# Other edge prices and durations in a kernel's own planner: scores behind scores, and the begins of GpSimd and VectorE pieces

## The chip, the cores and the metric

The kernel runs on one core of a Trainium2 chip. The metric is device time in microseconds (us) of one execution; lower is better. Times are medians of several executions.

## The reference, cut to what matters

32 sequences of 256 tokens with 128 channels pass through a feed-forward network (`ffn`), an attention over channels, and the same feed-forward network again, all in float32:

```python
x = x + 0.5 * ffn(layernorm(x))
x = x + channel_attention(layernorm(x))   # softmax(q^T k / sqrt(8)) over channels, 16 heads
x = x + 0.5 * ffn(layernorm(x))
# ffn: two layers of
h = shift_token(x)                        # second half of the channels from the token before
q, k, v = split(h @ wqkv)                 # 8 heads of 64
q, k = rotary_xpos(l2norm(q) * qs, l2norm(k) * ks)
x = x + local_attention(q, k, v) @ wo     # each block of 64 sees itself and the block before
h = layernorm(shift_token(x)) * lg + lb
a, g = split(h @ w1 + b1)
x = x + (a * gelu(g)) @ w2 + b2
```

## The kernel before

One sequence is two tiles of 128 tokens (t = 0 and 1). Each layer of each sequence is cut into pieces, each of which runs on one engine:

- `shifted_T` (L173): TensorE transposes the normalised x (L179), two copies put it into hT, one token late for half of the channels.
- `project` (L186): TensorE makes q and k (L198, 1024 columns, into a two-bank PSUM place called "wide") and v (L232, into a one-bank place called "bank"). ScalarE squares (L204), VectorE multiplies by the cosine and sine tables (L206, L209) and sums the squares (L215), GpSimd makes the norms (L219, L125), adds (L223) and scales (L226).
- TensorE transposes q and k (`transposed`, L141); ScalarE or VectorE copies them out (L131).
- `scores` (L240): TensorE writes the scores of one t into a "wide" place. They are 64 small matmuls on parts of the array (L264, 64 x 32) and a mask on the whole array (L252). For t = 0 the mask comes first, for t = 1 last. VectorE takes the maximum and subtracts it (L275, L278), ScalarE takes the exponential (L281).
- `attended` (L284): the probabilities are transposed (L141), 32 small products with the values go into a "wide" place (L303, parts of the array of 96 x 32), VectorE divides (L310, L311).
- `attention_out` (L318): a transpose (L141) and a product (L326), VectorE adds (L331).
- `gated_mlp` (L377): SP moves half of the channels by one token in three copies on chip (L381, L382); `layernorm` (L147) takes statistics on VectorE (L153, L154), their scale on GpSimd (L157 to L160) and the normalisation on ScalarE (L164); then z is transposed, TensorE makes three hidden pieces (L395), ScalarE the gelu (L403), VectorE the gate (L410), TensorE the output (L421).
- `channel_attention` (L451) is a chain of small products (L465, L477, L503) and a softmax.

There are two "wide" and four "bank" places in PSUM. Up to eight sequences are under way at once (`CHAINS`, L33).

No loop sets the order of the pieces. Class `Plan` (L656) does, when the kernel is built. Every `plan.op` names the engine, a duration in us, what it follows, and the places that it uses. `Plan.order` (L718) plays the pieces against clocks of its own for the five engines, looks 30 TensorE pieces ahead, tries 16 orders with small random delays, and keeps five pieces of the one with the least idle time of TensorE. Then each engine's instructions are issued in the order found, and semaphores do the waiting on the chip.

Three tables enter that play. `SYNC` (L663) is what an engine needs to begin after another engine's piece. `TAIL` (L664) is how long after a piece its result is there. `CHANGE` (L666) is added to TensorE's begin by the form that the array was left in and the form that the next piece begins with: "all", "parts" (scores) or "values". Scores of t = 0 have the form ("all", "parts"), scores of t = 1 ("parts", "all") (L273), attended values ("values", "values") (L307). `begin` (L776) adds it:

```python
t = max(o.given[engine], self.clock[engine] + self.CHANGE.get((self.array, o.form[0]), 0.0))
```

and `go` (L805) sums `t - self.clock["PE"]` up as TensorE's idle time, so that a negative entry counts as time won. The duration of t = 0 scores is given as 1.35 us and that of t = 1 scores as 1.16 (L272).

Of the kernel before, what the change touches and what calls it, by code (L numbers as in the profile page):

```python
# [40 lines left out]
def kernel(ctx: ExitStack, tc: tile.TileContext, ins: dict, out: bass.AP):  # L41
    nc = tc.nc
    x = ins["x"]
# [34 lines left out]
    plan = Plan()  # L78
# [45 lines left out]
    def rsqrt(dst, src, n):  # L124
        nc.gpsimd.tensor_tensor(dst, src, mhalf[:, :n], ALU.pow)  # L125
# [21 lines left out]
    def layernorm(src, x, kind, after):  # L147

        st, mv, var, rstd, shift, y = (plan.take(k) for k in ("st", "mv", "v1", "v1", "v1", kind))

        def stats(e):
            for t in range(NT):
                nc.vector.bn_stats(st.t[:, t, :], src(t))  # L153
                nc.vector.bn_aggr(mv.t[:, t, :], st.t[:, t, :])  # L154

        def scale(e):
            nc.gpsimd.tensor_scalar_add(var.t, mv.t[:, :, 1], EPS)  # L157
            rsqrt(rstd.t, var.t, NT)
            nc.gpsimd.tensor_mul(shift.t, mv.t[:, :, 0], rstd.t)
            nc.gpsimd.tensor_scalar_mul(shift.t, shift.t, -1.0)  # L160

        def norm(e):
            for t in range(NT):
                nc.scalar.activation(  # L164
                    y.t[:, t, :], src(t), AF.Identity, bias=shift.t[:, t : t + 1], scale=rstd.t[:, t : t + 1]
                )

        a = plan.op("DVE", 0.84, stats, after, [x, st, mv, var, rstd, shift, y])
        b = plan.op("POOL", 1.6, scale, [a], [mv, var, rstd, shift])
        c = plan.op("ACT", 0.79, norm, [b], [x, rstd, shift, y])  # L170
        return y, c
# [205 lines left out]
    def gated_mlp(l, y1, after):  # L377
# [5 lines left out]

        moved = plan.op("SP", 2.15, shift, after, [y1], late=2.0)
        z, n = layernorm(lambda t: y1.t[:, t, 0:2, :].rearrange("p a d -> p (a d)"), y1, "z", [moved])
        zT, uT, y2 = (plan.take(k) for k in ("zT", "uT", "y"))
        _, q = transposed(lambda: [z.t[:, t, :] for t in range(NT)], NT, lambda: zT.t, zT, [n], [z])
# [49 lines left out]
    def ffn(x, after):  # L437

        y, d = layernorm(lambda t: x.t[:, t, :], x, "y", after)
        for l in range(DEPTH):  # L440
            y1, done = local_attention(l, y, [d])
            y, d = gated_mlp(l, y1, done)
        xn = plan.take("x")
        e = plan.op(
            "DVE", 0.35,
            lambda e: nc.vector.scalar_tensor_tensor(xn.t, y.t, 0.5, x.t, ALU.mult, ALU.add), [d], [x, y, xn],
            apart=True,
        )
        return xn, [e]

    def channel_attention(x, after):  # L451


        xn, d = layernorm(lambda t: x.t[:, t, :], x, "y", after)
        xT = plan.take("xT")
        _, tr = transposed(lambda: [xn.t[:, t, :] for t in range(NT)], NT, lambda: xT.t, xT, [d], [xn])
# [142 lines left out]
    def make_hidden(l, after):  # L599

        pb = plan.take("bank")

        def mm(e):
            for a in range(2):
                for j, (c0, n) in enumerate(HCH):
                    i = a * len(HCH) + j
                    nc.tensor.matmul(
                        pb.t[:n, i : i + 1], w1[:, l, a * HID + c0 : a * HID + c0 + n],
                        lnb[:, l : l + 1], start=True, stop=True,
                    )  # L610

        def add(e):
            sums = pb.t[:, : 2 * len(HCH)].rearrange("p (a j) -> p a j", a=2)
            for n, js in ((P, slice(0, 2)), (HCH[2][1], slice(2, 3))):
                nc.vector.tensor_add(b1[:n, l, :, js], b1[:n, l, :, js], sums[:n, :, js])

        m = plan.op("PE", 2.0, mm, after, [pb])
        return [
            plan.op("DVE", 0.2, add, [m], [pb]),
            plan.op("DVE", 0.6, lambda e: nc.vector.tensor_scalar_mul(w1[:, l, :], w1[:, l, :], lng[:, l : l + 1]), [m], []),  # L620
        ]
# [3 lines left out]
    def prepare():  # L625

        raw = plan.take("qk")
        t = plan.op("ACT", 1.5, lambda e: load_tables(*tables(raw)), [], [raw], late=4.5)
        first = plan.op("SP", 0.5, lambda e: load_wqkv(0), [], [], late=6.0)
        cast = plan.op("DVE", 0.2, lambda e: nc.vector.tensor_copy(identh, ident), [], [])  # L630
        made["tables"] = [[make_tables(l, raw, [t])] for l in range(DEPTH)]
        made["masks"] = make_masks(made["tables"][0] + made["tables"][1] + [cast])
        plan.rank = 2.3
        hidden = plan.op("SP", 5.5, lambda e: load_hidden(), [], [], late=8.0)
        plan.rank = 3.3
        second = plan.op("SP", 0.5, lambda e: load_wqkv(1), [], [], late=6.0)
        rest = plan.op("SP", 3.0, lambda e: load_rest(), [], [], late=8.0)
        plan.rank = 0
        made["hidden"] = [make_hidden(l, ([hidden], [hidden, rest])[l]) for l in range(DEPTH)]
        made["weights"], made["more"] = [[first], [second]], [[hidden], [rest]]  # L640

    for g in range(x.shape[0]):
        plan.rank, plan.base = g, len(plan.ops)
        xt, seq = plan.take("x"), plan.take("sequence")
        a = plan.op("SP", 0.5, lambda e, xt=xt, g=g: nc.sync.dma_start(xt.t, xg[g]), [], [xt, seq], late=2.5)
        if g == 0:
            prepare()
        xo, a = ffn(xt, [a])
        xo, a = channel_attention(xo, a)
        xo, a = ffn(xo, a)  # L650
# [5 lines left out]
class Plan:  # L656
# [3 lines left out]

    SYNC = {"PE": 0.16, "DVE": 0.08, "ACT": 0.08, "POOL": 0.09, "SP": 0.08}  # L663
    TAIL = {"PE": 0.165, "ACT": 0.105, "DVE": 0.085, "POOL": 0.04, "SP": 0.0}  # L664

    CHANGE = {("all", "parts"): 0.09, ("all", "values"): 0.09, ("values", "values"): -0.11}  # L666
    RATHER = 1.0
    TABLE = 1.3
    TURNS = ("wide", "bank")
# [106 lines left out]
    def begin(self, o, engine):  # L776

        t = max(o.given[engine], self.clock[engine], self.clock["POOL"] if o.apart else 0.0)
        if engine == "PE":
            t = max(o.given[engine], self.clock[engine] + self.CHANGE.get((self.array, o.form[0]), 0.0))  # L780
        sync = self.SYNC[engine]
        for p in o.uses:
# [22 lines left out]
    def go(self, until, later, chance):  # L805
# [16 lines left out]
        while heap and (until is None or self.through < until):  # L822
# [44 lines left out]
            for d in o.then:  # L867
                self.undo.append((d, {"wait": d.wait}))
                d.wait -= 1
                if not d.wait:  # L870
                    d.given = {
                        e: max(x.done[0] + (self.SYNC[e] if x.done[1] != e or x.late else 0.03) for x in d.after)
                        for e in d.engines
# [52 lines left out]
```

## Time and profile before

| what | us |
|---|---|
| median of three timed runs | 2786.19 |
| their lowest and highest | 2784.39, 2789.49 |
| the profiled execution | 2782.01 |
| its span in the profile | 2780.2 |
| TensorE busy with matmuls | 2732.8 |
| GpSimd, VectorE, ScalarE busy | 2215.1, 2125.3, 1977.0 |

The mean granted TensorE clock of the span is 0.998. The profile shows one execution. Busy columns count instructions, not waits. Matmuls are pipelined: one begins before the one ahead of it has ended, so in a timeline the difference of two starts tells how long a piece holds TensorE, and the busy column (second figure) is longer than that. In a row of stretches, the columns after the stretch and its length are the busy time of TensorE's matmuls, its weight loads, VectorE, ScalarE and GpSimd, each with its count of instructions, then the granted clock, the share of the DMA engines and GB/s.

### The profile page before, as it was taken

The page shows a single profiled execution, that of the slowest core. Times are in us where ns is not written, and L with a number is a line of the kernel's source. Part 1 is how long each engine was busy: PE and PEld are TensorE (multiplying, and loading weights), DVE is VectorE, ACT ScalarE, POOL GpSimd, SP SyncE. Part 2 cuts the span into 40 slices and gives each one's busy share as a digit, 9 for nine tenths or more (in the row PEclk, how much of TensorE's full clock was granted, in tenths as well). Part 3 has the DMA queues.
Part 4 walks back from the last instruction along what each step waited for, and adds up shares of the span by engine and source line. Part 5 has one row for each costly group of instructions (what it writes and reads, how often), then busy time and mean ns, then how long its engine had stood idle before and what let it go on. Part 6 is the DMA issues. An engine that isn't in the chain of part 4 may idle for free.

```text
span 2780.2 us, 106518 instructions
## 1 busy us (share of the span) xinstructions
PE 2732.8 (98%) x46200; PEld 2116.9 (76%) x46200; DVE 2125.3 (76%) x3762; ACT 1977.0 (71%) x3595; POOL 2215.1 (80%) x1972
## 2 busy tenths in 40 slices
PE   7999999999999999999999999999999999999999
PEld 4777778778777777777877777777787777778677
DVE  6788777777787777777878778777877788776776
ACT  5777767767677777767677777677766677677666
POOL 8888887888787788787868979788779788684884
PEclk9999999999999999999999999999999999999999
DMA  3112111212112111112111121221111121111111
GB/s 104 40 36 53 41 44 44 54 38 64 42 41 53 34 40 49 48 41 55 44 50 39 38 52 50 52 53 43 38 48 41 47 52 46 43 49 31 41 48 40
DMA packets 125585, 129.68 MB, mean 47 GB/s; under 512 B 56592, under 2 KB 75452, under 8 KB 125116
## 3 DMA queue, kind: packets, MB, share of 16 engines
q1 hardware_dynamic: 124300, 122.47, 16.9%
q8 instruction: 363, 5.95, 0.9%
q14 instruction: 106, 0.87, 0.1%
q10 hardware_dynamic: 816, 0.39, 0.0%
HBM read 8.00 MB, written 4.19 MB: 4 GB/s over the span
## 4 chain that ended last, share of the span: by engine, by line
PE 92%; DVE 3%; POOL 2%; issue 1%; ACT 1%; DMA 1%; SPq 0%; POOLq 0%; DVEq 0%; ACTq 0%
PE ps_bank L141 21%; PE ps_wide L198 15%; PE ps_bank L395 11%; PE ps_wide L303 9%; PE ps_bank L326 8%; PE ps_wide L264 8%; PE ps_bank L232 7%; PE ps_bank L421 6%; PE ps_wide L252 3%; PE ps_bank L465 1%; PE ps_bank L179 1%; POOL rn L125 1%; PE ps_bank L503 1%; DMA y<-y 0%; DVE cp L494 0%
## 5 line engine op out<-in xcount | busy, mean ns | idle before, releaser
L223 POOL TENSOR_TENSOR qk<-qk,sq 128x1024 f32<-128x1024 f32 x256 | 606.8, 2371 | 243.3 <-DVE sq L209 120.6
L125 POOL TENSOR_TENSOR rn<-ssq,mhalf 128x16 f32<-128x16 f32 x256 | 748.4, 2923 | 21.3
L226 POOL TENSOR_TENSOR qk<-qk,rn 128x1024 f32<-128x1024 f32 x256 | 487.5, 1906 | 13.7
L198 PE MATMUL ps_wide<-wqkv,hT 128*128 128x512 f32 x1024 | 487.2, 598 | 2.9 <-DVE pr L278 2.1
L206 DVE TENSOR_TENSOR qk<-ps_wide,tab 128x1024 f32<-128x1024 f32 x256 | 312.3, 1220 | 191.9 <-ACT sq L204 115.4
L395 PE MATMUL ps_bank<-zT,w 128*128 128x256 f32 (+1 forms) x1536 | 372.9, 381 | 1.7 <-ACT zT L131 1.1
L204 ACT ACTIVATE sq<-ps_wide 128x1024 f32<-128x1024 f32 x256 | 262.4, 1025 | 140.0 <-PE ps_wide L198 93.3
L131 ACT COPY pT<-ps_bank 96x512 f32<-96x512 f32 x508 | 283.3, 585 | 93.8 <-PE ps_bank L141 89.1
L209 DVE TENSOR_TENSOR sq<-ps_wide,tab 128x1024 f32<-128x1024 f32 x256 | 311.0, 1215 | 45.2 <-PE ps_wide L198 28.4
L215 DVE TENSOR_REDUCE ssq<-sq 128x16 f32<-128x1024 f32 x256 | 309.7, 1210 | 35.0 <-ACT sq L204 34.6
L395 PEld LDWEIGHTS ps_bank<-zT,w 128*128 128x128 f32 (+1 forms) x1536 | 259.3, 178 | 64.5 <-issue 12.7
L198 PEld LDWEIGHTS ps_wide<-wqkv,hT 128*128 128x128 f32 x1024 | 180.7, 191 | 146.2 <-issue 134.8
L141 PE MATMUL ps_bank<-ident,qk 128*128 128x128 f32 x2048 | 286.0, 275 | 1.4 <-POOL qk L226 1.2
L275 DVE TENSOR_REDUCE mx<-ps_wide 128x8 f32<-128x768 f32 x256 | 242.9, 949 | 57.8 <-PE ps_wide L252 30.8
L141 PE MATMUL ps_bank<-ident,pr 128*96 128x128 f32 x2048 | 286.3, 274 | 0.3
L303 PE MATMUL ps_wide<-vm,pT 96*32 96x65 f32 x8192 | 273.8, 221 | 3.5 <-issue 2.5
L326 PEld LDWEIGHTS ps_bank<-wo,oT 128*128 128x128 f32 x2048 | 252.5, 192 | 29.4 <-issue 19.7
L303 PE MATMUL ps_wide<-vt,pT 96*32 96x65 f32 x8192 | 272.4, 220 | 1.8 <-issue 1.7
L326 PE MATMUL ps_bank<-wo,oT 128*128 128x128 f32 x2048 | 270.6, 276 | 0.8 <-ACT oT L131 0.8
L141 PEld LDWEIGHTS ps_bank<-ident,pr 128*96 128x96 f32 x2048 | 229.5, 126 | 48.7 <-issue 31.8
L232 PE MATMUL ps_bank<-wqkv,hT 128*128 128x512 f32 x512 | 261.3, 603 | 5.2 <-DVE uT L410 2.1
L141 PEld LDWEIGHTS ps_bank<-ident,qk 128*128 128x128 f32 x2048 | 234.8, 141 | 37.8 <-issue 20.9
(102 smaller groups left out, 5266.4 us busy)
## 6 DMA issues: line engine op xcount, KB each, us to landing
vm<-vt SPq DMA_DIRECT2D x256, 195.0 KB
vm<-vt SPq DMA_DIRECT2D x256, 130.0 KB
vm<-vt SPq DMA_DIRECT2D x256, 65.0 KB
y<-y SPq DMA_DIRECT2D x128, 56.0 KB
x<-in_x SPq DMA_DIRECT2D x32, 128.0 KB
out<-x SPq DMA_DIRECT2D x32, 128.0 KB
y<-y SPq DMA_DIRECT2D x128, 7.5 KB
y<-y SPq DMA_DIRECT2D x128, 0.2 KB
```

Of the source, the lines that this page charges most:

```text
L125: nc.gpsimd.tensor_tensor(dst, src, mhalf[:, :n], ALU.pow)
L141: nc.tensor.transpose(pt.t[:rows, j * P : (j + 1) * P], src, ident)
L198: nc.tensor.matmul(wide.t[:, a], lhsT(), wqkv[:, l, a * INNER : (a + 1) * INNER], start=True, stop=True)
L206: c = plan.op("DVE", 1.14, lambda e: nc.vector.tensor_mul(qk.t, pq(), cos), [m] + made["tables"][l], [wide, qk])
L209: lambda e: nc.vector.tensor_mul(sn.t.rearrange(five, x=2), pq().rearrange(five, x=2)[:, :, :, ::-1, :], sin.rearrange(five, x=2)),
L215: "DVE", 1.13, lambda e: nc.vector.tensor_reduce(ssq.t, sq.t, AX.X, ALU.add), [s], [sq, ssq]
L223: f = plan.op("POOL", 2.42, lambda e: nc.gpsimd.tensor_add(qk.t, qk.t, sn.t), [c, i], [qk, sn])
L226: lambda e: nc.gpsimd.tensor_mul(qk.t, qk.t, rn.t.unsqueeze(3).to_broadcast([P, 2, HEADS, DH])),
L232: lambda e: nc.tensor.matmul(mv.t, lhsT(), wqkv[:, l, 2 * INNER :], start=True, stop=True),
L303: nc.tensor.matmul(o()[q, r, j, :], pTs[r].t[:FR, j, q], v[:, 2 * j + r, :], start=True, stop=True)
L326: nc.tensor.matmul(pw.t[:, :P], oT.t[:, j, :], wo[:, l, j, :], start=j == 0, stop=j == PAIRS - 1)
L395: nc.tensor.matmul(pa.t[:w, i * SEQ : (i + 1) * SEQ], w1[:, l, i * HID + c0 : i * HID + c0 + w], zf(), start=True, stop=True,)
```

## The change

Five numbers of the planner are other ones. No piece, engine, tile or place is added or taken away; the planner finds another order with them, on every engine and in SP's queue. The statistics of `layernorm` are counted at 0.95 us instead of 0.84, the TensorE piece of `make_hidden` (twelve one-column products for the bias sums, run twice at the start) at 1.15 instead of 2.0, the begin of a GpSimd piece behind another engine's at 0.15 instead of 0.09, and scores that follow scores in the form "parts" have an entry of their own in `CHANGE`, where there was none (0.0).

```diff
-        a = plan.op("DVE", 0.84, stats, after, [x, st, mv, var, rstd, shift, y])
+        a = plan.op("DVE", 0.95, stats, after, [x, st, mv, var, rstd, shift, y])
...
-        m = plan.op("PE", 2.0, mm, after, [pb])
+        m = plan.op("PE", 1.15, mm, after, [pb])
...
-    SYNC = {"PE": 0.16, "DVE": 0.08, "ACT": 0.08, "POOL": 0.09, "SP": 0.08}
+    SYNC = {"PE": 0.16, "DVE": 0.08, "ACT": 0.08, "POOL": 0.15, "SP": 0.08}
...
-    CHANGE = {("all", "parts"): 0.09, ("all", "values"): 0.09, ("values", "values"): -0.11}
+    CHANGE = {("all", "parts"): 0.09, ("all", "values"): 0.09, ("values", "values"): -0.11, ("parts", "parts"): -0.18}
```

## The prediction

> **What bounds the kernel now.** I read the page first, for the bound; then the chain of waits on it; then the busy time by stretches; last TensorE's timeline, because the change is about single edges between TensorE pieces.
>
> ```profile
> span 2780.2 us, 106518 instructions
> PE 2732.8 (98%) x46200; PEld 2116.9 (76%) x46200; DVE 2125.3 (76%) x3762; ACT 1977.0 (71%) x3595; POOL 2215.1 (80%) x1972
> PE 92%; DVE 3%; POOL 2%; issue 1%; ACT 1%; DMA 1%; SPq 0%; POOLq 0%; DVEq 0%; ACTq 0%
> ```
>
> TensorE is busy 98% of the span and carries 92% of the chain that ended last; no other engine is above 80%. So time goes only if TensorE's own pieces follow each other faster, or if its waits shrink. Next, where TensorE waits (PE busy is the third figure of a row):
>
> ```profile
> 0.00:100.00 100.00, 83.58 (x1107) 55.98 (x1108) 65.53 (x125) 60.46 (x108) 86.77 (x127) 0.97 0.30 85
> 100.00:2500.00 2400.00, 2380.43 (x40685) 1850.68 (x40685) 1865.04 (x3268) 1728.10 (x3138) 1946.04 (x1673) 1.00 0.18 46
> 2580.00:2600.00 20.00, 17.87 (x130) 11.32 (x129) 13.52 (x27) 12.77 (x27) 18.52 (x21) 0.91 0.15 38
> ```
>
> Start: 16.4 us idle in 100. Middle: 19.6 idle in 2400. The last 280 us: 11.2 idle. The middle is nearly full, so waits there can hardly give more than some microseconds. What remains are the edges:
>
> ```profile
> 1002.56 1.00 PE L264 MATMUL ps_wide<-kT,qT 64*32 64x96 f32 x64
> 1003.49 1.08 PE L141 MATMUL ps_bank<-ident,pr 128*96 128x128 f32 x8
> ...
> 1016.27 1.88 PE L198 MATMUL ps_wide<-wqkv,hT 128*128 128x512 f32 x4
> 1017.99 0.60 PE L141 MATMUL ps_bank<-ident,ob 128*128 128x128 f32 x4
> ```
> ```profile
> 1005.27 1.88 PE L198 MATMUL ps_wide<-wqkv,hT 128*128 128x512 f32 x4
> 1007.08 0.75 PE L264 MATMUL ps_wide<-kT,qT 64*32 64x96 f32 x43
> ```
> ```profile
> 1090.07 1.73 PE L264 MATMUL ps_wide<-kT,qT 64*32 64x96 f32 x128
> 1091.73 0.39 PE L252 MATMUL ps_wide<-mask,identh 128*128 128x256 bf16 x2
> ```
>
> Read starts, not busy times. A first-half score block (t=0, it ends in the small array parts) that a transpose follows holds TensorE 0.93 us from its first L264 (1002.56 to 1003.49). A projection before a whole-array piece takes 1.72 (1016.27 to 1017.99); before a second-half score block (t=1, it begins in the parts) it takes 1.81 (1005.27 to 1007.08). At 1090 the two blocks stand together: 128 score matmuls take 1.66, where two apart take 2 x 0.93.
>
> **The edges, over all records.** From start to start, medians where nothing waits: the last matmul of t=0 to the next piece is 172 ns (117 edges), to a t=1 block 2 ns (11 edges). A t=1 block or an attended-values block costs 93 ns more to enter after a whole-array piece (202 against 109 after a transpose, 522 against 429 after a projection), and nothing more after a t=0 or a values block. Values to values is 36 ns, values to anything else 148, and the second of two such blocks is 24 ns shorter inside (876 against 900). So the new price of -0.18 is a real edge: 172 - 2 = 170 ns, and the pair saves the 93 of entry besides.
>
> **What the change does.** It adds and removes no matmul. It gives the planner another price for one edge and four other durations, and the whole order comes out otherwise. I counted the order of instructions of both kernels, which no run is needed for:
> - t=0 directly followed by t=1: 11 before, 58 after (of 128). +47 x 0.170 = **8.0 us** less.
> - values directly followed by values: 60 before, 74 after. +14 x (0.148 - 0.036 + 0.024) = **1.9 us** less.
> - entries from a whole-array piece into values or t=1: 278 before, 241 after. -37 x 0.093 = **3.4 us** less.
> - all other edges depend only on the piece before, and those are the same pieces.
>
> TensorE's unstalled work thus falls by **13.3 us**. Summed from edges and medians it was 2683.7 us of 2780.2, the rest being 9.7 before the first piece, 4.0 after the last matmul's start and 83 of stalls by starts (more than the idle columns show, since records overlap).
>
> **The other constants.** The statistics piece goes from 0.84 to 0.95 us; the trace has 2765.26 to 2766.23, or 0.97, so the new one is right. The bias sums' TensorE piece goes from 2.0 to 1.15; its twelve passes span 1.04 and an edge, right too. GpSimd's begin goes from 0.09 to 0.15. They act only through the order; I cost them at nothing of their own, hidden in a middle that idles 0.8%. Without that cover, 224 statistics pieces that are 0.11 late each bound them at 25 us of gain if every one stalled TensorE now; the stalls that I find end in other ways, so I take zero and 3 us at most.
>
> ScalarE's table loads fall from 170 to 160, 10 x 1283 ns = 12.8 us, on an engine busy 71%: nothing. Evacuations on VectorE go from 31 to 30: nothing.
>
> **Stalls, in three places.** The order decides how much TensorE work lies between a piece and what needs it. I compared these distances.
>
> Middle: the short distances hardly move. From projection to its transposes (2nd percentile) 11.3 before, 11.8 after; scores to transposes of the probabilities 4.0 and 4.2 (t=0), 3.6 and 3.8 (t=1); reuse of a two-bank place after t=1 2.8 and 2.8. Of the 47 us that TensorE loses there by starts, most is in scattered events of 1 to 2 us, which no distance foretells. I take 0, bounds -8 and +8.
>
> Start: the same pieces in nearly the same order up to the first scores. I take 0, bounds -3 and +5.
>
> End: here the orders differ in kind. Before, the last four sequences finish together: three transposes of z and nine hidden pieces of several sequences fill the last 15 us. After, sequence 31 comes last alone. Behind the transposes of its first queries every piece waits for the one before. The least distances that the trace of before shows: output projection to transposed z 8.3 to 9.0 us (through an add, SP's three shift copies, statistics, GpSimd, the normalisation), z to hidden 0.8, hidden to output 1.5, values to transposes 1.3, transposed probabilities to values 1.1, scores to transposes 3.4. Less what lies between in the new order, I get 17 to 18 us of stall in the last 50 us, 2.5 ahead of it, and 1 to 3 of small ones: 21 to 24, against 18.0 by starts over the last 280 us before. **+5 us**, bounds +2 and +11.
>
> The clock belongs here. After the 2.1 us of idle ahead of 2586.8 the granted clock is 0.91 over 2580 to 2600, and the twelve passes of L421 take 2.93 us where others take 1.50, 1.4 us lost:
>
> ```profile
> 2586.82 0.86 PE L179 MATMUL ps_bank<-ident,y 128*128 128x128 f32 x2 [2.13 <-ACT y L164]
> 2587.47 2.93 PE L421 MATMUL ps_bank<-w,uT 128*128 128x128 f32 x12
> ```
>
> One such spell after the idle of 8 us: **+2 us**, bounds +1 and +3. The Trainium skill (TensorE: Matmul & The Clock Gate, "What's actually happening") says that the clock halves after an idle window of about 3.4 us and needs about as long a busy one to return. By the page the idle ahead of 2586.8 was too short for that; this trace shows the drop all the same. By the page's window the last pieces would lose about 1.7 to 3.4 us, an estimate that leaves the sum where it is within 1.4.
>
> **The sum.** -13.3 + 0 + 0 + 5 + 2 = **-6.3 us**. The profiled execution took 2782.0 (span 2780.2, 1.8 around it), so 2775.7 by it. The timed runs' median is 2786.19, 4.2 above the profiled one; the difference carries over, so I predict 2780.
>
> **Rivals.**
> 1. *The end and the start give all of it back*: end +11 and clock +2, start 0. Sum 0, **2786**. For it: the lone last sequence, whose 8 to 9 us wait nothing can fill. Against: before loses 18 us in its end too. Chance 0.22.
> 2. *Both two-bank places in VectorE's queue* (slower). There are two such places, and each pair fills both. VectorE reads them one after the other, 949 + 950 ns each (L275, L278), so the second comes free 1.9 us later than if it had stood alone, and a projection or a values block behind it waits. It outweighs the gain from 6.3 / 47 = 0.13 us for each added pair; if one pair in four pays 1.9, that is 47 x 0.25 x 1.9 = 22 us, sum +16, **2802**. For it: the one pair that has a wait inside it (964.1, 2.2 us, released by L278) stalls just so. Against: 9 of the 11 pairs of before run within 15 ns, and the reuse distances did not shrink. Chance 0.20.
> 3. *Fewer stalls as well*: true prices, ten table loads fewer, middle -8 and end +1: -13.3 - 8 + 1 + 2 = -18, **2768**. For it: the constants do match the records. Against: the middle's big stalls aren't of that kind. Chance 0.15.
> 4. *The edge isn't saved*: the 2 ns comes from 11 edges only. Then -5.3 + 7, about +2, **2788**. Chance 0.03.
>
> The forecast has 0.40; three quarters of it lie below -5.6 us. About 0.2% (5.6 us) is what a measurement of this kernel can tell from no change. Faster: 0.30 + 0.15 = 0.45. Within: 0.10 + 0.22 + 0.03 = 0.35. Slower: 0.20. The range goes from the gain with best bounds (-13.3 - 8 - 3 + 2, about -22) to +14, half of rival 2 left out: 2764 to 2800.
>
> **What would show it.** 58 places with 128 score matmuls on end and L264's starts 0.74 us apart there; table loads 160; TensorE's last 50 us with an idle of 8 us or more ahead of the last L141 of z, and a clock below 1 behind it; the middle's PE idle near 20 us per 2400. Wrong if the middle's idle grows by 10 us or more with L278 as the releaser (rival 2), or if the end's idle stays near 11 us.

## The result and the profile after

The changed kernel takes 2773.03 us (median of 4, 2771.74 to 2775.54), the kernel before 2787.84 beside it. The ratio is 0.9947, 95% interval 0.993 to 0.9965: 14.8 us faster, where 6.3 were forecast. The profiled execution of the changed kernel took 2775.54 us; by the profiled execution of before (2782.01) I had computed 2775.7.

The page of the changed kernel, the same three lines as before:

```profile
span 2773.7 us, 106474 instructions
PE 2719.2 (98%) x46200; PEld 2115.8 (76%) x46200; DVE 2119.9 (76%) x3761; ACT 1958.2 (71%) x3586; POOL 2217.3 (80%) x1972
PE 92%; DVE 3%; POOL 2%; DMA 1%; issue 1%; ACT 1%; SPq 0%; ACTq 0%; POOLq 0%; DVEq 0%
```

TensorE is busy 13.6 us less with the same 46200 matmuls, and the span is only 6.5 shorter. The stretches tell where the rest went; the second fence is the kernel before, over a last stretch of the same length:

```profile
0.00:100.00 100.00, 81.83 (x1089) 53.85 (x1090) 66.45 (x125) 57.29 (x106) 86.58 (x127) 0.97 0.31 87
100.00:2494.00 2394.00, 2378.47 (x40891) 1860.18 (x40891) 1862.73 (x3294) 1728.87 (x3160) 1949.53 (x1687) 1.00 0.18 46
2720.00:2774.00 54.00, 36.92 (x425) 27.70 (x423) 22.93 (x45) 20.50 (x36) 18.93 (x20) 0.87 0.10 28
```
```profile
2726.00:2780.00 54.00, 49.21 (x915) 42.19 (x913) 31.50 (x72) 31.68 (x59) 19.43 (x24) 1.00 0.17 42
```

Idle at the start: 18.2 us against 16.4. In the middle: 15.5 against 19.6. In the last 54 us: 17.1 against 4.8, and the granted clock there is 0.87 against 1.00. TensorE's timeline of that end (matmuls of L303 and the last rows left out):

```profile
2753.44 1.16 PE L326 MATMUL ps_bank<-wo,oT 128*128 128x128 f32 x8 [0.68 <-ACT oT L131]
2761.30 0.86 PE L141 MATMUL ps_bank<-ident,z 128*128 128x128 f32 x2 [6.71 <-ACT z L164]
2762.63 4.77 PE L395 MATMUL ps_bank<-zT,w 128*128 128x256 f32 x12 [0.46 <-ACT zT L131]
```

The lone last sequence waits 6.7 us for its z, and the twelve hidden passes behind it take 4.77 us, most of them at a halved clock; twelve of them take 2.75 where the clock is full (at 1010.70 in the kernel before). The records show half of the clock for 10.2 us, from 2756.3 on. That is 1.7 us into the idle time; in the 3.4 us up to there TensorE had been idle for 2.25. The Trainium skill (TensorE: Matmul & The Clock Gate, "What's actually happening") has the clock halved after an idle window of about 3.4 us. This trace agrees with the length (spells of half a clock last 3.4, 6.8 or 10.2 us) and not with the condition: no spell of the changed kernel between 100 us and its last matmul needed 3.4 us of idle to begin, 1.6 to 2.25 were enough.

An added pair of score blocks, and an idle time of another kind right behind one:

```profile
1539.43 1.81 PE L264 MATMUL ps_wide<-kT,qT 64*32 64x96 f32 x128
1541.17 0.39 PE L252 MATMUL ps_wide<-mask,identh 128*128 128x256 bf16 x2
1541.40 0.61 PE L326 MATMUL ps_bank<-wo,oT 128*128 128x128 f32 x4
1543.89 0.60 PE L326 MATMUL ps_bank<-wo,oT 128*128 128x128 f32 x4 [1.88 <-issue]
```

The 128 score matmuls take 1.74 us from the first to the mask (1.66 in the pair shown of before, 2 x 0.93 apart). Over all 58 pairs the median from the last matmul of t = 0 to the first of t = 1 is 1 ns; the 70 blocks that stand alone still pay 173. The 1.88 us in front of the second half of L326 are put down to "issue": no semaphore that the profile shows ends them.

### The profile page after: what moved, and what is told of

It is laid out like the page before. It is cut to its first block, busy times and chain, and to the rows that moved or that the text cites. A ratio compares the mean times of both kernels' runs of the same rounds, so it can differ in the third digit from the quotient of the medians.

```text
span 2773.7 us, 106474 instructions
## 1 busy us (share of the span) xinstructions
PE 2719.2 (98%) x46200; PEld 2115.8 (76%) x46200; DVE 2119.9 (76%) x3761; ACT 1958.2 (71%) x3586; POOL 2217.3 (80%) x1972
## 4 chain that ended last, share of the span: by engine, by line
PE 92%; DVE 3%; POOL 2%; DMA 1%; issue 1%; ACT 1%; SPq 0%; ACTq 0%; POOLq 0%; DVEq 0%
PE ps_bank L141 21%; PE ps_wide L198 15%; PE ps_bank L395 12%; PE ps_wide L303 9%; PE ps_bank L326 8%; PE ps_wide L264 8%; PE ps_bank L232 7%; PE ps_bank L421 6%; PE ps_wide L252 3%; PE ps_bank L465 1%; PE ps_bank L179 1%; DMA y<-y 1%; POOL rn L125 1%; PE ps_bank L503 1%; POOL qk L223 0%
## 5 line engine op out<-in xcount | busy, mean ns | idle before, releaser
L395 PEld LDWEIGHTS ps_bank<-zT,w 128*128 128x128 f32 (+1 forms) x1536 | 261.3, 179 | 71.2 <-issue 18.6
L326 PEld LDWEIGHTS ps_bank<-wo,oT 128*128 128x128 f32 x2048 | 253.0, 192 | 30.7 <-issue 21.4
L326 PE MATMUL ps_bank<-wo,oT 128*128 128x128 f32 x2048 | 271.7, 276 | 3.8 <-issue 2.6
L303 PE MATMUL ps_wide<-vt,pT 96*32 96x65 f32 x8192 | 270.3, 220 | 4.6 <-issue 4.2
L303 PE MATMUL ps_wide<-vm,pT 96*32 96x65 f32 x8192 | 270.6, 221 | 0.3 <-issue 0.3
```

Of the source, the lines that this page charges most:

```text
L303: nc.tensor.matmul(o()[q, r, j, :], pTs[r].t[:FR, j, q], v[:, 2 * j + r, :], start=True, stop=True)
L326: nc.tensor.matmul(pw.t[:, :P], oT.t[:, j, :], wo[:, l, j, :], start=j == 0, stop=j == PAIRS - 1)
L395: nc.tensor.matmul(pa.t[:w, i * SEQ : (i + 1) * SEQ], w1[:, l, i * HID + c0 : i * HID + c0 + w], zf(), start=True, stop=True,)
```

## The experiments

By "stall" I mean, as in the prediction, the sum over TensorE's pieces of what their starts lie later than the medians of the unstalled ones. It holds one thing that is no wait: a whole-array piece right behind a block of small matmuls is slower in its first pass (shown with the edges below), which makes some 20 us of the stall of the kernel before and 17 of the changed one's. Microseconds against before are ratios taken with the kernel before on the same chip.

**1 and 11: the same order without the pairs' saving.** The scores of t = 0 write the mask last:

```diff
...
-            if t == 0:
-                mask()
             for j in range(PAIRS):
...
-                            kT.t[row, j, k0 : k0 + FR], start=t == 1 and j == 0, stop=t == 0 and j == PAIRS - 1,
+                            kT.t[row, j, k0 : k0 + FR], start=j == 0, stop=False,
...
-            if t == 1:
-                mask()
+            mask()
```

> The changed kernel with every engine's order kept, but the scores of t = 0 write their mask after the score matmuls, as those of t = 1 do, so no block ends in the array's parts and the 58 pairs no longer share them. Edges theory (the gain is the edges): each pair pays 0.170 + 0.093 us again, 58 x 0.263 = 15.3 us on TensorE with the same order, so about 16 us above the changed kernel: 2788. Rival (the gain is luck of the new order or fewer waits, the edges lie in slack): 2773 to 2777. Half of each (stalls absorb part of the longer edges): 2780.

Measured: 2779.29, ratio 0.9981 (0.9972 to 0.9989). Then again, beside the changed kernel itself:

> The changed kernel's order with the mask of t = 0 last, beside the changed kernel on one chip. Edges theory: 15 us above it. Theory from the first look at this pair (TensorE's score pieces take 18 us more and its waits elsewhere 17 less, so the edges are paid back as waits): 1 to 7 us above it.

Measured: 2777.47 (ratio 0.9974, 0.9963 to 0.9985) against 2768.12 for the changed kernel: **9.4 us**, between the two theories. One pair in both, the changed kernel first (in the other kernel the scores stand at L262):

```profile
1301.90 0.49 PE L252 MATMUL ps_wide<-mask,identh 128*128 128x384 bf16 x2
1302.32 1.73 PE L264 MATMUL ps_wide<-kT,qT 64*32 64x96 f32 x128
1303.98 0.39 PE L252 MATMUL ps_wide<-mask,identh 128*128 128x256 bf16 x2
1304.21 0.38 PE L179 MATMUL ps_bank<-ident,y 128*128 128x128 f32 x2
```
```profile
1309.15 1.00 PE L262 MATMUL ps_wide<-kT,qT 64*32 64x96 f32 x64
1310.08 0.50 PE L252 MATMUL ps_wide<-mask,identh 128*128 128x384 bf16 x2
1310.51 1.00 PE L262 MATMUL ps_wide<-kT,qT 64*32 64x96 f32 x64
1311.44 0.39 PE L252 MATMUL ps_wide<-mask,identh 128*128 128x256 bf16 x2
1311.67 0.38 PE L179 MATMUL ps_bank<-ident,y 128*128 128x128 f32 x2
```

From the block's start to the transpose it is 2.31 us with the pair and 2.52 without, and 0.09 of entry lies ahead of it: 0.30 in all, and 0.298 by the medians of the 58 pairs, where 0.263 were computed. Piece by piece over the whole order, the pieces with scores, and those just ahead of them, take 17.7 us longer than in the changed kernel on that chip. But the edit does one thing more than it was meant to: no t = 0 block ends in the array's parts now, and so the 69 whole-array pieces behind a block that stands alone take 57 ns less in the median, 4.9 us in all. The other 3127 pieces take 1.1 less. So the edges are worth a little more than was computed, and in these two profiles hardly any of it comes back as waits: the spans are 11.7 us apart, the medians 9.4. Run 1 against the first profile of the changed kernel gives 18.2 longer, 4.8 less and 12.3 less; that profile has 7.4 us more stall than the one of run 10.

**2: another end, the order ahead of it kept.**

```diff
+            if at == total // self.STRETCH * self.STRETCH - 300:
+                chance = random.Random(9)
             sight = at + self.SIGHT if at + self.SIGHT < total else None
```

> The changed kernel, with the planner's random generator seeded anew when some 300 TensorE pieces are left; the order ahead of that is the same, and at the end the last sequences finish together instead of sequence 31 alone. Theory that the lone last sequence costs the end some 10 us (28 us of stall by starts in the last 280 us, against 18 before): 8 to 14 us below the changed kernel, 2759 to 2765. Rival (the end is bound by a chain that no order shortens): within 3 us of 2773.

Measured: 2749.3, ratio 0.9879 (0.9864 to 0.9893). The changed kernel has 0.9947, so this is 0.0068 or 19 us less, more than the 8 to 14 expected, and it beats both kernels. Its last 54 us:

```profile
2694.00:2748.00 54.00, 48.65 (x792) 41.89 (x790) 32.01 (x70) 32.47 (x62) 20.62 (x24) 0.98 0.13 34
```

5.4 us idle where the changed kernel has 17.1. Stall over the last 280 us is 11.0 against 28.2, that is 17.2 of the 19; the edges of the new end give 1.3.

**3 and 4: the price alone, the durations alone.** The first adds only the entry in `CHANGE`, the second only the three other constants.

> The kernel before with only the new price of scores behind scores. The order has 42 such pairs, 58 values behind values, 260 entries: 6.6 us less TensorE work than before by edges. Edges theory: 2781, with some 6 us either way for stalls. Rival (the durations make the gain): 2788.

Measured: 2767.81, ratio 0.9945 (0.9932 to 0.9958).

> The kernel before with only the three other constants (statistics, bias sums, begin of GpSimd). 8 pairs, 70 values behind values, 273 entries: 1.3 us less by edges. Edges theory: 2786, with some 6 us either way for stalls. Rival (truer durations mean fewer waits): about 2775.

Measured: 2761.07, ratio 0.9923 (0.9908 to 0.9937). Each alone gains as much as both or more, and each lies below all that was expected of it: the edges give 6.6 of 17 us in the first and 1.3 of 24 in the second. With the durations alone TensorE's unstalled work is 2682.6 us, nearly that of before, and the stall 62.2 against 83.5. That looks like true durations shrinking the waits, but the next four speak against it.

**5 to 8: other seeds of the planner's random generator**, with the constants of before (5, 6) and of the change (7, 8).

```diff
-        at, chance, kept = 0, random.Random(1), {}
+        at, chance, kept = 0, random.Random(2), {}
```

> The kernel before with another seed of the planner's random generator (2), all constants as before: how far luck of the order alone moves the time. By edges 0.7 us more work than before. Luck theory (the 24 us of the durations alone are mostly luck of one order): the four seeded kernels of this call spread by 10 us or more within a set of constants, and this one may lie anywhere from 2765 to 2800. Constants theory (true durations shrink the waits): this one stays within 5 us of before, 2780 to 2790.

> As the run with seed 2, with seed 3. By edges 1.4 us less work than before. Luck theory: 2765 to 2800, and 10 us or more from seed 1 or 2. Constants theory: 2780 to 2790.

> The changed kernel with seed 2. By edges 11.3 us less work than before and 2.7 more than the changed kernel; at the end the last sequences finish together and not one alone. Theory of edges plus end: 10 us below the changed kernel for the end, 3 above for the edges, about 2766. Luck theory: anywhere from 2750 to 2785. Rival that the change is worth nothing but by luck: above 2780.

> The changed kernel with seed 3. 49 pairs, 54 values behind values, 265 entries: by edges 7.5 us less than before, 4.7 more than the changed kernel. Theory of edges plus end: about 2768 if its end is as short as before's. Luck theory: 2750 to 2785. Rival that the change is worth nothing but by luck: above 2780.

| constants, seed | us | ratio to before | unstalled TensorE work | stall |
|---|---|---|---|---|
| before, 1 | 2787.84 | 1 | 2683.7 | 83.5 |
| before, 2 | 2770.74 | 0.9954 (0.9939 to 0.9969) | 2684.5 | 71.2 |
| before, 3 | 2759.5 | 0.991 (0.9894 to 0.9927) | 2682.5 | 64.5 |
| changed, 1 | 2773.03 | 0.9947 (0.993 to 0.9965) | 2670.7 | 91.2 |
| changed, 2 | 2766.45 | 0.9936 (0.9921 to 0.9951) | 2673.2 | 80.5 |
| changed, 3 | 2772.64 | 0.9958 (0.9943 to 0.9973) | 2676.7 | 83.4 |

The luck theory holds for the old constants: without any change of them the time moves by 25 us. The three seeds of the new ones lie within 6 us, less than the 10 that it asked for. The mean ratio is 0.9955 for the old constants and 0.9947 for the new ones. Unstalled work is 10.0 us less in the mean (2683.6 and 2673.5), and the stall 12 more (73.1 and 85.0). With the slower first passes counted as work, the work is 12.7 less and the waits are 14.6 more. The edges are saved with each seed, and waits take the saving up. Three seeds a side can't tell what is left of it from nothing.

**9 and 10: both kernels again**, unchanged.

> The kernel before itself, for the spread between executions: one profiled pair gave 2782.0 before and 2775.5 after (6.5 apart), the timed medians are 14.8 apart. If the profiled execution of before was a fast draw, this profile lies above it, 2782 to 2790, and the ratio to before is 1.000 within 0.001.

Measured: 2783.21, ratio 1.0001 (0.9991 to 1.0011), and a profile of 2779.28, not the 2782 or more that I expected.

> The changed kernel itself, on the same chip as the next two. If the medians are right and the profile was a slow draw: 12 to 16 us below before, profile 2770 to 2774. If the profiled pair is right: 6 to 8 us below before.

Measured: 2768.12, ratio 0.9943 (0.9931 to 0.9954), profile 2768.12. So the medians are right: about 15 us. Two profiles of the same changed program differ by 7.4 us, and by the same 7.4 in stall (91.2 and 83.8), 6.4 of it in the middle. About 3.4 us of it are waits put down to "issue" (those of 0.3 us or more, after the first 100 us: 10.9 and 7.5). Its end is alike both times: 16.4 us idle in the last 54, clock 0.87.

**12: half of the instructions in the values blocks of t = 0.** One product for the three blocks of 32 rows that read the same 96 rows of values:

```diff
-                    for b in range(NB):
-                        q = slice(b * BLK, (b + 1) * BLK)
+                    for b, n in ((0, 3), (3, 1)) if t == 0 else ((0, 1), (1, 1), (2, 1), (3, 1)):
+                        q = slice(b * BLK, (b + n) * BLK)
```

> The changed kernel's order, but the values of t = 0 use one product of 96 columns for the three blocks that read the same 96 rows: 16 products instead of 32, half of the instructions of that block. Theory that the waits which no semaphore ends (12 us in the middle, all at or behind the second of two dense blocks) are the supply of instructions: such waits behind two values blocks with one of t = 0 go, 4 to 8 us less than the changed kernel, unless the block itself gets longer (its time is read from the trace; 0.1 us each is 13 us). Rival (they are tied to the place in the program or to the clock): the same waits stand at the same pieces.

Measured: 3324.05, ratio 1.1957 (1.1932 to 1.1983). The block got longer, from about 1.05 us to 4.27 by starts:

```profile
1004.20 0.31 PE L303 MATMUL ps_wide<-vt,pT 96*96 96x65 f32 x2
1004.43 0.30 PE L303 MATMUL ps_wide<-vm,pT 96*32 96x65 f32 x2
1004.66 0.38 PE L303 MATMUL ps_wide<-vt,pT 96*96 96x65 f32 x2
1004.98 0.30 PE L303 MATMUL ps_wide<-vm,pT 96*32 96x65 f32 x2
```

Products of 96 and of 32 columns alternate, and each change of form takes 150 to 178 ns from start to start, where the products of a plain block begin some 14 ns apart. The Trainium skill (TensorEngine Tiling (Array Packing), "Key Properties") says that a change of tiling mode drains TensorE; the trace shows a price at each change of form, in line with that, and can't show whether it is a drain. For its own question the run is **inconclusive**. TensorE's waits put down to "issue" nearly vanish, but in a kernel that is 550 us slower, at a mean granted clock of 0.943, much else has time to catch up. The changed kernel's waits in the middle first, then this kernel's:

```profile
PE ps_wide L303 <- issue: 4.5, 4, 1.6
PE ps_bank L326 <- issue: 2.6, 2, 1.9
PE ps_wide L264 <- issue: 1.6, 2, 0.8
PE ps_bank L465 <- DVE cp L494: 1.5, 2, 1.2
```
```profile
PE ps_bank L465 <- DVE cp L494: 1.5, 2, 1.2
PE ps_bank L465 <- ACT vt L131: 0.9, 1, 0.9
PE ps_bank L141 <- issue: 0.8, 2, 0.6
```

## Why the prediction came out as it did

- **The edges, -13.3.** Right in sign and mechanism, some 4 us too small. The 58 pairs stand in the trace at 1 ns, and TensorE's busy time fell by 13.6. By starts alone the work fell by 17.1 (for each piece the median step to the next one, by its kind, by whether small parts stand before it, and by the form that follows). What the sum left out is in its sentence "all other edges depend only on the piece before": the first pass of a whole-array piece is 41 to 103 ns longer behind small parts than behind another whole-array piece (10 for a mask), and the order has 278 such places before and 241 after, 2.6 us less. The rest is inside the pairs. Two outputs of run 10, the first behind a projection, the second behind a values block:

```profile
1003.64 1.50 PE L421 MATMUL ps_bank<-w,uT 128*128 128x128 f32 x12
1010.25 1.61 PE L421 MATMUL ps_bank<-w,uT 128*128 128x128 f32 x12
```

It is not a gain of 17 us in the time: run 11, without the pairs' saving, costs 9.4 on the clock while its edit gives 4.9 back by itself, and over three seeds nothing certain is left.

- **The other constants, 0.** Not settled. Alone they gain 24 us by the medians beside them (2784.96 and 2761.07), but two seeds with no constant changed gain 13 and 25. I can't tell their part from luck.
- **Middle, 0 (-8 to +8).** In its bounds, at their edge in one pair: stall fell from 49.6 to 45.3 in the first pair of profiles and from 49.1 to 38.9 in the second. Some 3 us of each fall are cheaper first passes and pairs and belong to the edges; 1.6 and 7.2 are left. Of the 47 us that the prediction calls lost there, some 18 are such passes and not events of 1 to 2 us. What went most of the waits are those for the softmax of the channel attention (L494, 3.6 us of idle to 1.5 in both pairs) and for L278 (3.0 to 0.5 and to none). Nothing that I counted in the order foretold it.
- **Start, 0.** 1.8 us more by stall, 2.7 in the second pair: in its bounds.
- **End and clock, +5 and +2.** Right in mechanism, a little small: +10.2 (18.0 to 28.2) in both pairs. The lone sequence came as read from the order, the wait for z was 6.9 us by starts and not 8 to 9, since every engine is free there, and the halved clock came twice, for 3.4 us at 2732.4 and for 10.2 us at 2756.3.
- **The sum.** By the profiled execution -6.5 against -6.3 forecast, which is luck as well: the work gave 17.1 and not 13.3 and the middle 1.6, while the start took 1.7 and the end 3 more than forecast. What failed most is the step "the difference carries over". The profiled execution of before lay 4.2 us under its median, that of the changed kernel 2.5 above its own. These 6.7 us are most of the 7 between 2780 and 2773; in run 10 the profile of the changed kernel is its median. The profile of before lay under the median on both occasions (2782.0 and 2779.3 against 2787.8 and 2783.2); why is open.
- **Rivals.** 1 (the end gives all back) had the right place, but the edges and the middle gave more than it took. 2 (both two-bank places in VectorE's queue) did not come: waits of TensorE for L278 in the middle fell. 3 (fewer stalls too) is nearest in time, with a shorter middle as it said but a longer end. 4 is refuted by the 58 edges. None of them had the mechanism that the seeds show: any change of the order moves the stalls by some 20 us, more than the edges that the change is about.

## What to carry to other kernels

When a planner's constants change, its whole order does. Run a few seeds of the old constants first, since their spread is the noise that the change has to beat (25 us here, for an edge saving of 17). Fixing the order and taking the one saving away tells what that saving is worth on the clock (9 us here), if you also look at what else the edit makes cheaper. Then read the end of the order: one sequence left alone at the end cost 12 us of idle more in the last 54 us, and another draw of the end alone was worth more than the change.

## What the runs showed of the hardware

- An edge between array forms: scores (64 x 32) to a whole-array piece 172 to 173 ns, scores to scores 1 to 2 ns, into small parts from the whole array 93 ns more than into a whole-array piece; 96-column and 32-column products in turn 150 to 178 ns. Behind small parts the first pass of a whole-array piece takes longer besides: 41 to 57 ns for transposes, 102 for most float32 products.
- Waits of TensorE that no semaphore ends, up to 2.0 us of idle each, stand at or behind blocks of small matmuls. In the thirteen profiles other than run 12's there are 93 of 0.3 us or more after the first 100 us; in 90 of them two or more of these blocks are among the five pieces that end with the one that waited, where 15 to 19% of all pieces have that. Some recur at the same piece in runs of the same order (the one ahead of 1543.89 us was 1.88, 1.12 and 1.13 us in the changed kernel, run 10 and run 2), others don't (1.47 us at 1254.7 is in neither of these two). A supply of instructions that can't keep up would do that, since one block is 64 matmuls and 64 weight loads within 1 us, but it is only argued: run 12 did not settle it.
- The granted clock fell to half after 2.1 us of idle in the kernel before, and in the changed one after 1.9 us (at 1544.6, behind the wait shown above) and inside the idle time of 6.7 us; the last of these cost twelve hidden passes 2.0 us. Each spell between the first 100 us and the last matmul of both kernels began behind 3.4 us of which TensorE was idle for 1.6 to 2.3.
